# A four-layer residual block with paged attention: old rows kept together, a new passage between two parts, the end in halves, and the first tile's weights in chunks

## The chip, the cores and the metric

One core of one Trainium2 chip runs the whole program in one launch. The metric is device microseconds of one execution; the time of a kernel is the median of its runs.

## The reference

The input x has 64 sequences of 64 tokens with 512 features, float32. Four layers follow one another, each added to its input:

```
x = x + (x @ W0[id[b]] + b0[id[b]])                  # one of 16 experts for each sequence b
x = x + (x @ W1.T + scal[a] * (x @ A[a].T) @ B[a].T) # one of 8 adapters a of rank 16 for each sequence
q, k, v = x @ Wq.T, x @ Wk.T, x @ Wv.T               # 8 query heads, 4 key heads of 64
q, k = rope(rms(q)), rope(rms(k))                    # positions kv_len[b] + t
write k, v into a paged cache (blocks of 16 rows, 257 entries in the table of each sequence)
x = x + softmax(mask(q . k_cache / 16)) . v_cache @ Wo.T    # window of 256 positions
x = x + (x^T mixed over t by w3[subject[b]] (64 x 64) + bias)
```

All blocks of the table are read after all new rows are written, so a sequence can see rows that another one has just written. Products are float32 throughout.

## The kernel before

**Tiles.** The 4096 tokens are 32 tiles of 128, each of two sequences. A tile is kept once with features on partitions (for products) and once with tokens on partitions. The program is written out in order for each engine; the engines run their own instructions in that order and wait for one another where data is needed. SP issues most DMAs in program order; GpSimd (POOL) issues the gathers.

**Part 1** runs layers 0 and 1 and the q, k and v products, over groups of 1, 1, 2 and then seven times 4 tiles (`GROUPS`). For a tile, `layer0` (L254) multiplies both sequences by their expert's weights (1 MB each, `load_w0`, L237), 16 matmuls; ACT copies the result (L257), TensorE transposes it (`turn0`, L278), and DVE adds it (L279) to x plus bias, which POOL has made (`add_bias`, L265) from `biasT`, a transpose of the gathered bias rows `brow` (L683, L684). `layer1` makes the adapter's inner product (`pxa`, L630) and scales it (L635), multiplies by W1 plus the identity (L645; the identity is added to `w1` at L403), and adds the adapter's outer product (L653). The sum x2 is copied (L658), written to DRAM and transposed (`turn_x2`, L664). `product` (L141) makes q (`pq`) and k, v (`pk`). `turned` normalises and rotates q and k by `gains`, made from the sine and cosine of `rotation(o)`, eight tiles at a time (L375 to L397; 26 instructions of DVE, two of ACT). `keep_kv` writes the new k and v rows into `kvd` (L673), a compact copy of the cache in DRAM; `turn_q` (L175, L182) transposes q and writes it to `qTd`. Tile i+2 is loaded by `load_next(i)` after the first layer of tile i.

Two generators run beside this: `windows` makes the indices and masks of the cache rows that each sequence needs, and `copies` brings the 17 old blocks of each of the 64 sequences into `kvd`: 68 gathers by POOL into buffers `st` (L155, pool `op`, six buffers) and 68 writes of 512 KB by SP (L162). A write follows three gathers after its own. `other` and `layer1` advance them; up to seven gathers come in a group of four tiles. A set of 16 sequences is spread over the partitions by selection matmuls (`pw`, L488), so that one write is contiguous in DRAM.

**Passage.** Part 1 makes the q products of the first 27 tiles, and `LATE` = 6 keeps x2 of the last ones for the time after it: four products in a loop (tiles 27 to 30), the last in the first step of part 2. Meanwhile POOL gathers the cache rows of the first tiles (`load_kv`, L767, five gathers for a tile), SP loads masks (`mb`), queries (`qT`) and Wo.

**Part 2** takes one tile a step: `scores` (L839, with mask and row maximum on DVE at L847 and the exponential on ACT at L851), `attend` (L886) for the tile before, `normalise` (L859, L863), `project` (L909, residual added at L913) for the tile two before, `keys` (transposes of k and of the new rows, L820 to L827), `turn` (transposes of the weights, L872 to L876). `last(i)` does the last layer for a pair of tiles (`pz`, L921; activation with the bias, L928) and writes the output. After the loop, the last tiles are finished in the order below.

```
    last(i - 3)
    attend(i)
    project(i)
    last(i - 1)
```

## Time and profile before

| | us |
|---|---|
| median of 7 runs | 983.77 |
| runs | 978.08, 981.76, 983.44, 983.77, 984.80, 985.09, 986.80 |
| profiled execution | 988.38 |
| its span | 986.5 |
| TensorE busy | 934.1 (95%) |
| VectorE, ScalarE, GpSimd busy | 608.7, 412.5, 405.5 |
| mean granted TensorE clock | 0.986 |

The span is the time from the first to the last record on the core; all times of the profile count from its start. PE is TensorE, DVE VectorE, ACT ScalarE, POOL GpSimd, SP SyncE. `L254` is line 254 of the kernel before. In the timelines an entry has its start, its length, the operation and, in brackets, the idle time of the engine ahead of it with what ended it. The DMA share is the mean busy share of the 16 DMA engines of the core.

### The profile page before, as it was taken

The numbers are of one execution on the slowest core, as the hardware profiler recorded it, in microseconds if no ns is written. First come the engines' busy times: TensorE is split into PE (matmuls) and PEld (weight loads), VectorE is DVE, ScalarE is ACT, GpSimd is POOL, SyncE is SP. The second block draws the span as 40 slices with busy tenths as digits, with TensorE's granted clock in tenths as the row PEclk, the third lists the DMA queues.
The fourth block names the chain that finished last, engine by engine and source line by source line (L and its number), as shares of the span: only waits on it lengthen the run. The fifth ranks groups of instructions, "written<-read, shape, count | busy, mean of one in ns | idle before, by whom it ended". The sixth has DMA issues, their size and how long they took to land.

```text
span 986.5 us, 17774 instructions
## 1 busy us (share of the span) xinstructions
PE 934.1 (95%) x5393; PEld 503.8 (51%) x5393; DVE 608.7 (62%) x1737; ACT 412.5 (42%) x1082; POOL 405.5 (41%) x600
## 2 busy tenths in 40 slices
PE   3999999998999999999999589999999999999997
PEld 1444444444444444444444266666666666666663
DVE  5563988888583362542425576666666777666672
ACT  1112143222341333422223475666666666666661
POOL 2332466464353453544425443444444433333300
PEclk9899999999999999999999799999999999999999
DMA  8967999999999999999866756666665565555621
GB/s 291 305 224 263 356 370 327 403 356 352 375 313 397 385 324 406 357 361 399 297 248 216 250 179 202 201 201 200 200 197 191 181 200 186 191 183 193 201 59 43
DMA packets 133280, 260.97 MB, mean 265 GB/s; under 512 B 32801, under 2 KB 41378, under 8 KB 133186
## 3 DMA queue, kind: packets, MB, share of 16 engines
q1 hardware_dynamic: 109074, 179.66, 51.5%
q0 software_dynamic: 23280, 79.84, 24.1%
q8 instruction: 43, 0.70, 0.3%
q10 hardware_dynamic: 832, 0.35, 0.1%
q14 instruction: 51, 0.42, 0.1%
HBM read 190.29 MB, written 69.50 MB: 263 GB/s over the span
## 4 chain that ended last, share of the span: by engine, by line
PE 71%; DVE 3%; ACT 1%; DMA 1%; another core or an unknown queue 1%; issue 1%; POOL 0%; ACTq 0%; DVEq 0%
PE py L909 12%; PE ps L839 8%; PE po L886 8%; PE p L645 7%; PE pk L141 7%; PE pq L141 7%; PE p L254 6%; PE ppt L872 6%; PE pkt L820 2%; PE pz L921 2%; PE ppt L876 2%; PE pkt L826 1%; DVE pT L873 1%; PE px L664 1%; PE pqt L175 1%; PE pt L278 1%
## 5 line engine op out<-in xcount | busy, mean ns | idle before, releaser
L767 POOL DMA_INDIRECT kv<-kvd,idxn x128 | 126.4, 988 | 209.6 <-PE po L886 151.3
L851 ACT ACTIVATE pr<-pr,mx 128x320 f32<-128x320 f32 x256 | 140.1, 548 | 5.1 <-DVE mx L847 1.4
L254 PE MATMUL p<-w,xt 128*64 128x512 f32 x512 | 121.6, 612 | 13.4 <-DMA w<-in_W 13.4
L909 PE MATMUL py<-wo,oT 128*128 128x512 f32 x256 | 118.4, 605 | 1.6 <-DVE oT L904 0.8
L847 DVE CUSTOM_DVE_ANT_0 pr<-ps,mb 128x320 f32<-128x320 f32 x256 | 107.8, 486 | 14.1 <-remote 8.1
L645 PE MATMUL p<-w,x 128*128 128x512 f32 x256 | 115.6, 609 | 0.0
L141 PE MATMUL pk<-wkv,x 128*128 128x512 f32 x256 | 115.1, 594 | 0.6 <-ACT x L666 0.6
L141 PE MATMUL pq<-wq,x 128*128 128x512 f32 x256 | 115.6, 596 | 0.0
L839 PE MATMUL ps<-kT,qT 64*128 64x320 f32 x512 | 89.2, 470 | 19.2 <-DVE pT L873 10.4
L279 DVE TENSOR_TENSOR x<-pt,x 128x512 f32<-128x512 f32 x32 | 22.0, 689 | 129.5 <-PE pt L278 107.2
L136 POOL TENSOR_TENSOR qr<-qn,sq 128x512 f32<-128x512 f32 x27 | 34.3, 1269 | 157.0 <-DVE qn L135 157.0
L155 POOL DMA_INDIRECT st<-in_kvc,cidx x68 | 68.4, 1006 | 58.3 <-DMA kvd<-st 46.3
L873 DVE COPY pT<-ppt 128x512 f32<-128x512 f32 x64 | 41.6, 686 | 79.1 <-PE ps L839 37.9
L863 DVE TENSOR_SCALAR pr<-pr,sm 128x320 f32<-128x320 f32 x256 | 85.2, 394 | 2.2
L886 PE MATMUL po<-pT,kv 128*64 128x128 f32 (+1 forms) x1536 | 82.1, 278 | 0.0
L645 PEld LDWEIGHTS p<-w,x 128*128 128x128 f32 x256 | 49.0, 195 | 60.5 <-issue 59.4
L886 PEld LDWEIGHTS po<-pT,kv 128*64 128x64 f32 (+1 forms) x1536 | 68.9, 135 | 19.9 <-DVE mx L847 13.1
L909 PEld LDWEIGHTS py<-wo,oT 128*128 128x128 f32 x256 | 46.0, 189 | 62.7 <-issue 60.0
L254 PEld LDWEIGHTS p<-w,xt 128*64 128x64 f32 x512 | 34.9, 139 | 82.4 <-issue 66.5
L141 PEld LDWEIGHTS pq<-wq,x 128*128 128x128 f32 x256 | 46.5, 191 | 48.8 <-issue 47.9
L839 PEld LDWEIGHTS ps<-kT,qT 64*128 64x128 f32 x512 | 44.3, 189 | 52.9 <-DVE pT L873 29.2
L141 PEld LDWEIGHTS pk<-wkv,x 128*128 128x128 f32 x256 | 46.4, 190 | 48.5 <-issue 47.3
(186 smaller groups left out, 1313.3 us busy)
## 6 DMA issues: line engine op xcount, KB each, us to landing
w<-in_W SPq DMA_DIRECT2D x64, 1024.0 KB
kvd<-st SPq DMA_DIRECT2D x68, 512.0 KB
xt<-in_xT SPq DMA_DIRECT2D x32, 256.0 KB
x2d<-x2n SPq DMA_DIRECT2D x32, 256.0 KB
kvd<-kvn SPq DMA_DIRECT2D x32, 256.0 KB
qTd<-qTs SPq DMA_DIRECT2D x32, 256.0 KB
qT<-qTd SPq DMA_DIRECT2D x32, 256.0 KB
x2r<-x2d SPq DMA_DIRECT2D x32, 256.0 KB
```

The costliest lines, as they stand in the source:

```text
L141: TE.matmul(ps, x2s[i][:, c, :], w[:, c, :], start=c == 0, stop=c == KC - 1)
L155: P.indirect_dma_start(out=st, out_offset=None, in_=a["kvc"].rearrange("(n r) d -> n (r d)", r=2), in_offset=bass.IndirectOffsetOnAxis(ap= ...
L254: TE.matmul(p0[hs, :], xs[i][:, c, hs], w0s[i][h][:, c, :], start=c == 0, stop=c == KC - 1)
L645: TE.matmul(p1[i], x1s[i][:, c, :], w1[:, c, :], start=c == 0, stop=False)
L767: P.indirect_dma_start(out=kv[:, n, :], out_offset=None, in_=kvd, in_offset=bass.IndirectOffsetOnAxis(ap=at, axis=0),)
L839: TE.matmul(ps[g2][:, :NPOS], qT[rows, gp, b2].rearrange("p h t -> p (h t)"), kT[rows, gp, b2 * NPOS : (b2 + 1) * NPOS], start=True, stop= ...
L847: V.tensor_tensor_reduce(out=p, in0=ps[g2][:, :NPOS], in1=mb[:, b2, :], scale=-1.0, scalar=3.0e38, op0=ALU.add, op1=ALU.min, accum_out=mx[ ...
L851: S.activation(p, p, AF.Exp, bias=mx[:, g, b2 : b2 + 1], scale=-1.0, accum_out=sm[:, g, b2 : b2 + 1],)
L863: V.tensor_scalar(p, p, sm[:, g, b2 : b2 + 1], None, ALU.mult)
L872: TE.transpose(pt[:, n * 128 : (n + 1) * 128], pr[:, g, at : at + 128], ident)
L886: TE.matmul(po[b2][g2 * 64 : (g2 + 1) * 64, gp * 128 : (gp + 1) * 128], kv[rows, n, (G + g) * HD : (G + g + 1) * HD], pT[rows, c, m * 128 ...
L909: TE.matmul(py, oT[:, c].rearrange("p b t -> p (b t)"), wo[:, c, :], start=c == 0, stop=c == KC - 1)
```

## The change

It has four pieces. (1) The old rows: a gather takes, for block position j, row pair q (of four) in each half of the block, for all 64 sequences at once; no selection matmul is needed, and the 128 row pairs of a write (4 KB each) lie 136 rows (278 KB) apart in `kvd`. `op` and `xp` have five buffers instead of six. (2) The passage: `LATE` is 8, so six q products stand in the loop and two fewer in part 1; a q transpose follows the next product; the product of tile 31 stands in the first step in a bank of another pool, its normalisation in the second, and the last q transposes come in the first, fourth and fifth step. (3) The end: the projection of tile 30 uses a bank of the ring, attention of tile 31 comes ahead of the last layer of tiles 28 and 29, and projection, last layer and output of tile 31 are done in two column halves. (4) The head: the first tile's two weight blocks come in four chunks each, one block by SP's queue and one by ACT's; the transpose of the bias comes first; `rotation(0)`, the identity in `w1`, the q weights, four adapter rows and the mask (`um`, now `far`) come later.

The diff, cut:

```diff
-NSET = 4
...
-LATE = 6
+LATE = 8
...
-    cidx = const.tile([128, NSET * JOLD], I32, name="cidx")
+    cidx = const.tile([128, JOLD, BLOCK // 4], I32, name="cidx")
...
-    def product(i, w, name):
-        ps = bank(name)
+    def product(i, w, name, pool=None):
+        ps = pool.tile([128, 512], F32, name="py") if pool else bank(name)
...
-    def copies(sets, to, pool, ahead):
+    def copies(to, pool, ahead):
...
-        for s in sets:
-            for n in range(s * JOLD, (s + 1) * JOLD):
+        to = to.rearrange("(p j q r) d -> p j q (r d)", p=128, q=BLOCK // 4, r=2)
+        for j in range(JOLD):
+            for q in range(BLOCK // 4):
...
-                    in_offset=bass.IndirectOffsetOnAxis(ap=cidx[:, n : n + 1], axis=0),
+                    in_offset=bass.IndirectOffsetOnAxis(ap=cidx[:, j, q : q + 1], axis=0),
...
-                m = n - sets[0] * JOLD
-                waiting.append((to[m * 256 : (m + 1) * 256].rearrange("(p r) d -> p (r d)", r=2), st))
+                waiting.append((to[:, j, q], st))
...
-        xp = pa.enter_context(tc.tile_pool(name="xp", bufs=6))
+        xp = pa.enter_context(tc.tile_pool(name="xp", bufs=5))
...
-        op = pa.enter_context(tc.tile_pool(name="op", bufs=6))
+        op = pa.enter_context(tc.tile_pool(name="op", bufs=5))
...
-        kvi = su.tile([128, 1], I32, name="kvi")
-        tabi = su.tile([128, NBLK], I32, name="tabi")
-        for h in range(2):
-            hs = slice(h * B, (h + 1) * B)
-            nc.scalar.dma_start(kvi[hs], a["toks"][:, 3 * B :].rearrange("o b -> b o"))
-            nc.scalar.dma_start(tabi[hs], a["tab"])
...
-        def load_w0(i):
+        def load_w0(i, parts=1, queues=(nc.sync, nc.sync)):
...
-            for b in (2 * i, 2 * i + 1):
+            for b, queue in zip((2 * i, 2 * i + 1), queues):
...
-                r = nc.sync.value_load(tok1[0:1, 0, b : b + 1], min_val=0, max_val=E - 1)
-                nc.sync.dma_start(
-                    w, a["W0"][bass.ds(r, 1)].rearrange("a (c p) o -> p (a c) o", p=128)
-                )
+                r = queue.value_load(tok1[0:1, 0, b : b + 1], min_val=0, max_val=E - 1)
+                for n in range(parts):
+                    cs = slice(n * KC // parts, (n + 1) * KC // parts)
+                    queue.dma_start(
+                        w[:, cs], a["W0"][bass.ds(r, 1)].rearrange("a (c p) o -> p (a c) o", p=128)[:, cs]
+                    )
...
-        load_w0(0)
+        load_w0(0, KC, (nc.sync, nc.scalar))
...
+        load_a(0, range(2, 4))
...
-        load_weight(wq, "wqT")
-        load_a(0, range(2, 8))
+        kvi = su.tile([128, 1], I32, name="kvi")
+        tabi = su.tile([128, NBLK], I32, name="tabi")
+        for h in range(2):
+            hs = slice(h * B, (h + 1) * B)
+            nc.scalar.dma_start(kvi[hs], a["toks"][:, 3 * B :].rearrange("o b -> b o"))
+            nc.scalar.dma_start(tabi[hs], a["tab"])
...
-            for c in range(KC):
-                cs = slice(c * 128, (c + 1) * 128)
-                V.tensor_tensor(w1[:, c, cs], w1[:, c, cs], ident, ALU.add)
-
...
-        P.iota(oldr, pattern=[[0, 3], [JOLD * 256, NSET], [2, B // NSET]],
-               base=0, channel_multiplier=0, allow_small_or_imprecise_dtypes=True)
+        P.iota(oldr, pattern=[[0, 3], [JOLD * BLOCK // 2, B]], base=0, channel_multiplier=0,
+               allow_small_or_imprecise_dtypes=True)
+        half4 = su.tile([128, BLOCK // 4], F32, name="half4")
+        for h in range(2):
+            P.iota(half4[h * B : (h + 1) * B], pattern=[[1, BLOCK // 4]], base=h * BLOCK // 4, channel_multiplier=0,
+                   allow_small_or_imprecise_dtypes=True)
...
-        inset = su.tile([B, 128], F32, name="inset")
-        P.iota(inset, pattern=[[0, BLOCK // 2], [1, B // NSET]], base=0, channel_multiplier=0,
-               allow_small_or_imprecise_dtypes=True)
...
-            sel = su.tile([B, NSET, 128], F32, name="sel")
-            for k in range(NSET):
-                V.tensor_scalar(
-                    sel[:, k, :], inset, pidxf[:B], -float(k * B // NSET), ALU.subtract, ALU.is_equal
-                )
-            yield
-            yield
-            pw = bank("pw")
-            for k in range(NSET):
-                TE.matmul(pw[:, k * JOLD : (k + 1) * JOLD], sel[:, k, :], wt[:B, :JOLD], start=True, stop=True)
-            V.tensor_scalar(cidx, pw[:, : NSET * JOLD], BLOCK / 2.0, p16f, ALU.mult, ALU.add)
+            V.scalar_tensor_tensor(
+                cidx, bc(wt[:, :JOLD, None], [128, JOLD, BLOCK // 4]), BLOCK / 2.0,
+                bc(half4[:, None, :], [128, JOLD, BLOCK // 4]), ALU.mult, ALU.add,
+            )
...
-                ((4, None, ALU.logical_shift_right), 256.0),
-                ((1, BLOCK // 2 - 1, ALU.logical_shift_right, ALU.bitwise_and), 2.0 * B / NSET),
-                ((1, None, ALU.bitwise_and), 1.0),
+                ((3, 1, ALU.logical_shift_right, ALU.bitwise_and), B * JOLD * BLOCK / 2.0),
+                ((4, None, ALU.logical_shift_right), BLOCK / 2.0),
+                ((BLOCK // 2 - 1, None, ALU.bitwise_and), 1.0),
...
-        bg, old, turns, asked, made = windows(), copies(range(NSET), kvd, op, 3), {}, [], []
+        bg, old, turns, asked, made = windows(), copies(kvd[:OLD], op, 3), {}, [], []
...
-        run(rotation(0))
         scalars()
         biasT = su.tile([128, KC, B], F32, name="biasT")
-        layer0(0, False)
         pb = bank("pb")
         for c in range(KC):
             TE.transpose(pb[:, c * B : (c + 1) * B], brow[:, c * 128 : (c + 1) * 128], ident[:B, :B])
         S.copy(biasT.rearrange("p c b -> p (c b)"), pb[:, : KC * B])
-        add_bias(0)
+        layer0(0)
         turn0(0)
         load_next(0)
-
-        um = su.tile([128, NM], F32, name="um")
-        for h in range(2):
-            P.iota(um[h * 64 : (h + 1) * 64], pattern=[[1, NM]], base=0, channel_multiplier=-1,
-                   allow_small_or_imprecise_dtypes=True)
-        V.tensor_scalar(um, um, -0.5 * (WINDOW - 1), None, ALU.add)
-        V.tensor_tensor(um, um, um, ALU.mult)
-        V.tensor_scalar(um, um, 0.25 * WINDOW * WINDOW, NEG, ALU.is_gt, ALU.mult)
-        nc.sync.dma_start(maskd, um)
+        load_weight(wq, "wqT")
+        load_a(0, range(4, 8))
+
+        for c in range(KC):
+            cs = slice(c * 128, (c + 1) * 128)
+            V.tensor_tensor(w1[:, c, cs], w1[:, c, cs], ident, ALU.add)
+
+        def far():
+
+            um = su.tile([128, NM], F32, name="um")
+            for h in range(2):
+                P.iota(um[h * 64 : (h + 1) * 64], pattern=[[1, NM]], base=0, channel_multiplier=-1,
+                       allow_small_or_imprecise_dtypes=True)
+            V.tensor_scalar(um, um, -0.5 * (WINDOW - 1), None, ALU.add)
+            V.tensor_tensor(um, um, um, ALU.mult)
+            V.tensor_scalar(um, um, 0.25 * WINDOW * WINDOW, NEG, ALU.is_gt, ALU.mult)
+            nc.sync.dma_start(maskd, um)
+
         tiles = [list(range(t, t + n)) for t, n in zip(T0, GROUPS)]
...
+            if g == 0:
+                run(rotation(0))
+            elif g == 1:
+                far()
...
-            if i % 2 == 0:
+            if i % 2 == 0 or i == NT - 1:
...
+
...
-    def project(i):
-        py, oT = pyp.tile([128, 512], F32, name="py"), oTs.pop(i)
-        for c in range(KC):
-            TE.matmul(
-                py, oT[:, c].rearrange("p b t -> p (b t)"), wo[:, c, :], start=c == 0, stop=c == KC - 1
-            )
+    def project(i, ring=False, parts=1):
+        py, oT = bank("py") if ring else pyp.tile([128, 512], F32, name="py"), oTs.pop(i)
...
-        V.tensor_tensor(x3, py, pairs[i][0], ALU.add)
+        for p in range(parts):
+            fs = slice(p * D // parts, (p + 1) * D // parts)
+            if p:
+                py = bank("py")
+            for c in range(KC):
+                TE.matmul(
+                    py[:, fs], oT[:, c].rearrange("p b t -> p (b t)"), wo[:, c, fs],
+                    start=c == 0, stop=c == KC - 1,
+                )
+            V.tensor_tensor(x3[:, fs], py[:, fs], pairs[i][0][:, fs], ALU.add)
...
+    def last_one(i, parts):
+
+        x3, w3 = x3s.pop(i), pairs.pop(i)[1]
+        for p in range(parts):
+            fs = slice(p * D // parts, (p + 1) * D // parts)
+            pz = bank("pz")
+            for h in range(2):
+                hs = slice(h * T, (h + 1) * T)
+                TE.matmul(pz[hs, fs], w3[hs, :T], x3[hs, fs], start=True, stop=True)
+            res = bp.tile([128, D], F32, name="res", bufs=3)
+            S.activation(res[:, fs], pz[:, fs], AF.Identity, bias=w3[:, T:])
+            nc.sync.dma_start(out[i * 128 : (i + 1) * 128, fs], res[:, fs])
+
...
     for i in range(NT - LATE + 1, NT - 1):
         pq = product(i, wq, "pq")
+        parts[i] = parts_q(i, pq, V, cs[i])
+        next(parts[i])
         if i > NT - LATE + 2:
             turn_q(i - 2)
-        parts[i] = parts_q(i, pq, V, cs[i])
-        next(parts[i])
         if i - 1 in parts:
             run(parts.pop(i - 1))
         next(parts[i])
     keys(0)
-    turn_q(NT - 3)
     for s in range(NT):
         if s + 2 < NT:
...
             attend(s - 1)
         else:
-            pq = product(NT - 1, wq, "pq")
-        if s:
-            normalise(s, 0)
-        if s == 0:
-            run(parts.pop(NT - 2))
-            parts = parts_q(NT - 1, pq, V, cs[NT - 1])
-            normalise(s, 0)
-            next(parts)
-            next(parts)
+
+            parts[NT - 1] = parts_q(NT - 1, product(NT - 1, wq, "pq", pyp), V, cs[NT - 1])
+            turn_q(NT - 3)
+        normalise(s, 0)
+        if s == 1:
+            next(parts[NT - 1])
+            next(parts[NT - 1])
         normalise(s, 1)
         if s % 2 == 0 and s >= 4:
...
         if s + 1 < NT:
             keys(s + 1)
-        else:
-            project(s - 1)
-        if s == 0:
-            turn_q(NT - 2)
+        if s in (3, 4):
+            turn_q(NT - 5 + s)
         turn(s)
-        if s == 0:
-            run(parts)
-        elif s == 1:
-            turn_q(NT - 1)
+        if s in (2, 3):
+            run(parts.pop(NT - 4 + s))
     i = NT - 1
     load_pair(i)
     add_one(i - 1)
     add_one(i)
+    project(i - 1, ring=True)
+    attend(i)
     last(i - 3)
-    attend(i)
-    project(i)
-    last(i - 1)
+    last_one(i - 1, 1)
+    project(i, ring=True, parts=2)
+    last_one(i, 2)
```

## The prediction

> **What bounds the kernel now.** I read the page's busy times first, then the windows by stage, then TensorE's own timeline in the stages that showed gaps, then GpSimd's waits.
>
> ```profile
> PE 934.1 (95%) x5393; PEld 503.8 (51%) x5393; DVE 608.7 (62%) x1737; ACT 412.5 (42%) x1082; POOL 405.5 (41%) x600
> ```
>
> TensorE is busy for 934.1 of 986.5 us, so a change that keeps the arithmetic can only win inside the remaining 52.4 us, plus what a slow clock costs. The windows say where those lie:
>
> ```profile
> 0.00:12.00 12.00, 0.00 (x0) 0.00 (x1) 6.53 (x26) 1.28 (x1) 4.18 (x15) 1.00 0.64 181
> 12.00:30.00 18.00, 14.40 (x36) 5.47 (x37) 10.53 (x45) 1.69 (x4) 6.68 (x13) 0.84 1.05 389
> ...
> 100.00:400.00 300.00, 297.46 (x1158) 132.75 (x1156) 203.73 (x402) 88.72 (x197) 148.04 (x230) 0.99 1.00 365
> 530.00:548.00 18.00, 14.63 (x41) 6.46 (x39) 12.03 (x27) 5.87 (x16) 8.75 (x10) 1.00 0.82 276
> 548.00:560.00 12.00, 4.22 (x20) 2.59 (x22) 3.05 (x8) 2.58 (x6) 6.29 (x8) 0.58 0.84 318
> ...
> 957.00:987.00 30.00, 22.70 (x168) 12.26 (x164) 10.95 (x35) 8.77 (x23) 0.51 (x2) 0.94 0.15 44
> ```
>
> The second number is the length, the third TensorE's busy time; the last three are granted clock, DMA share and GB/s. Part 1 from 100 to 400 us leaves TensorE 2.5 us idle, with the DMA engines at a share of 1.00. The gaps are the head (12 us, then 3.6), the passage (3.4, then 7.8, with a clock of 0.58) and the end (7.3). The change touches exactly these three, and the copies inside part 1.
>
> **The head.** TensorE's timeline:
>
> ```profile
> 12.00 1.97 PE L254 MATMUL p<-w,xt 128*64 128x512 f32 x2 [12.00 <-DMA w<-in_W]
> 15.38 6.36 PE L254 MATMUL p<-w,xt 128*64 128x512 f32 x14 [1.42 <-DMA w<-in_W]
> 24.97 1.92 PE L630 MATMUL pxa<-x,ao 128*32 128x128 f32 x8 [1.89 <-DVE x L279]
> 26.82 5.82 PE L645 MATMUL p<-w,x 128*128 128x512 f32 x8
> ```
>
> A weight block is 1 MB and lands whole: the first matmul starts at 12.00 and the third waits for the second block until 15.38. Each of the 14 takes 6.36/14 = 0.454 us; sixteen of the same later take 3.65 us, 0.228 each, so this stretch runs at half rate. Then the bias: its transpose stands behind the layer's matmuls, GpSimd's addition ends after 24, and TensorE waits 1.89 us.
>
> With chunks, the two 256 KB pieces of one input chunk are enough for two matmuls. The stream does not grow: 3.1 MB had moved by 14.5 us, which holds both blocks and the tile, so the last pieces land by about 14.5 to 15. The bias rows landed at about 11 (the packets of their gather run from 9.0 to 11.0), and the transpose of the bias now comes first, so about 11.2 opens TensorE. Sixteen matmuls at half rate are 16 x 0.454 = 7.3, end 18.5, with the last pieces in time. Then copy 0.3 and transpose 0.66, addition 0.7 without the wait: layer 1's first product near 19.5 to 20 instead of 24.97, 5.2 earlier. Its eight big matmuls took 5.82 us at half rate against 3.65 later; the clock came back at 31.1, 19 us after the first matmul. Starting one earlier without the 1.42 and 1.89 gaps, it should come back inside that product; this gives up to 2.2.
>
> What is moved behind it costs something. The rotation (DVE 7.75 to 16.2, 8.45 us, until now under the wait for weights) now runs after layer 1 of tile 0, and the first steps of the index work (27.28 to 33.13, some 5.5 us with its picks) follow it on DVE, ahead of tile 1's x addition. From 20.5: 8.45 and 5.5 end at 34.5, addition 35.2. TensorE has until then the product 3.65 and 1.12, layer 0 of tile 1 3.65, two transposes 1.3, the k/v product 3.7: it would arrive at about 34 and wait 1.1. ScalarE's copy for tile 1 stands behind the sine and cosine of that rotation: another 1.0. So 5.2 + 2.2 - 2.1 = 5.3 gained by layer 1 of tile 1. Bounds: 9 if the waits are covered by the k/v product, 1 if the clock stays low through tile 0 and the bias rows land late in the fuller stream. The weight loads behind (k/v 1 MB, q 1 MB, adapter rows) are used after 38 us; the q load and four adapter loads go behind the load of tile 2, whose weights are then earlier. The DVE addition into w1 (0.9) moves behind tile 0's x addition and is needed only 1.9 us later: nothing. The mask work of 1.9 us on DVE (25.45 to 27.28) moves one group on, where DVE waited 5.7 us for TensorE at 38.8: nothing.
>
> The Trainium skill, "DMA: Bandwidth & Descriptors", Bandwidth, speaks against pieces: it asks for 1 MiB per transfer (341 GB/s) and has 138 GB/s at 64 KB. By an estimate from that page at the middle, 240 GB/s, two blocks need 8.7 us instead of 6.1, and the last pieces come 2.6 us later, at 17.5: the chain would still end at 18.4. I go by the row: several transfers share the engines, at 389 GB/s and a share of 1.05. The same page, "Issuing engines are not separate DMA queues", says that a second issuing engine saves only issue time; by the trace that is the 1.23 us between SyncE's two weight issues (3.47 and 4.70), and by that rule the second engine alone is worth at most this.
>
> **The passage.** TensorE's timeline again:
>
> ```profile
> 548.18 0.66 PE L820 MATMUL pkt<-ident,kv 128*128 128x128 f32 x4 [2.63 <-DMA kv<-kvd,idxh]
> ...
> 559.00 3.57 PE L839 MATMUL ps<-kT,qT 64*128 64x320 f32 x12 [7.29 <-ACT kT L827]
> 562.50 4.23 PE L141 MATMUL pq<-wq,x 128*128 128x512 f32 x8
> ...
> 570.73 1.25 PE L872 MATMUL ppt<-ident,pr 128*128 128x128 f32 x8 [1.59 <-DVE pr L863]
> ```
>
> The idle entries of 530 to 590 add to 14.4 us: 0.19 + 0.73 + 2.63 + 0.31 + 7.29 + 1.59 + 0.51 + 0.24 + 0.16 + 0.77. The last k/v product ended at 528.9, and the first gathered rows that needed it landed at 548.14, 19.3 us later. Between stood four q products. With LATE 8 there are six: 6 x 3.6 + 5 x 0.44 = 23.8 us, so 4.5 to spare, and the 2.63 goes. TensorE's total is unchanged, since the two products (8.1 us with their transposes) leave part 1. Each q transpose now comes behind the next product: 0.19, 0.73 and 0.31 go. The 7.29 is the doubtful one. ScalarE's copy of the keys and DVE's first masked score both start near 558.4 though their operands were ready by 552, and the burst of gathers, masks, queries and Wo (about 400 GB/s) drains at 557.8, 28.9 us after the last k/v product. If the stall belongs to the burst's end, TensorE now reaches the second scores at 23.8 + 1.1 + 1.4 = 26.3, and 2.6 of it stays. If it belongs to the old order (keys, query transpose and scores close together), all of it goes. The third case is among the rivals. The 1.59 stays, since half 1 of the normalisation of tile 1 still stands behind a q rotation with its table load, as do small ones: 3.5 altogether. Cold matmuls at 562.5 (4.23 for 3.60) give 1.0 back. Gain 14.4 - 3.5 + 1.0 = 11.9, or 9.3 with the rest of the stall. I take 10.5.
>
> **The end.**
>
> ```profile
> 965.48 3.70 PE L909 MATMUL py<-wo,oT 128*128 128x512 f32 x8 [0.78 <-DVE x L913]
> 975.72 3.70 PE L909 MATMUL py<-wo,oT 128*128 128x512 f32 x8 [0.84 <-DVE oT L904]
> 979.35 1.98 PE L921 MATMUL pz<-x,w 64*64 64x512 f32 x8
> ```
>
> From 961 on: projection of 29 3.7, turn 2.5, projection of 30 3.7 (a bank of its own, so the 0.78 goes), attention 2.6, the last layers of 28, 29 and 30 1.6 (they cover the 0.84), projection of 31 3.7 in halves, then half a last layer 0.6: about 979.3 instead of 981.35. The last activation is half of 0.69, and what follows it (982.1 to 986.5) stays. Gain 2.5; 1 if halves cost as much as wholes, 3.5 if the last activation's issue gap goes as well.
>
> **The copies.** The gathers stay 68, and so do the bytes. Four selection matmuls and DVE's wait of 3.8 us for them go, which TensorE feels as 0.6 at most. The writes are still of 4096 B per packet, 159 ns in the trace both for scattered reads and for contiguous writes, so rows 278 KB apart should cost nothing: I take 0; a tenth more per packet would be 68 x 128 x 16 ns / 16 = 8.7 us of DMA time, of which up to all shows where the share is 1.00. Five buffers instead of six:
>
> ```profile
> POOL st L155 <- DMA kvd<-st: 46.3, 12, 9.0
> ```
>
> GpSimd waits longer for a write. I put a burst 3 us later, and the x bias addition behind it has about 7.5 us to spare (it ended at 256.7 in one group and was needed at 264.2). I take 1 us in all; 5 if some groups overrun.
>
> **Sum.** 5.3 + 10.5 + 2.5 + 0.6 - 1 = 17.9. The profiled execution took 988.4 us (span 986.5), so 970.5 for one like it. It stands 4.6 above the median of 983.8; if the 7.29 stall is partly what made it long, ordinary runs gain less, so I subtract half of the 4.6: 968.
>
> **The rivals.** (a) *The stall stays* or was never in ordinary runs: the gain is 17.9 less 5.9 = 12, 972 to 976. For it: nothing in the profile names a releaser, only "remote". Against: both engines stall together while the DMA burst ends. (b) *The head does not come forward*: bias rows behind eight weight pieces, or the rotation in front of tile 1 is as long as what it freed; head gain 1, so 972 to 974. For it: DVE has 14 us of work in a row where TensorE has some 13.5. (c) *Slower: GpSimd late in part 1.* With five buffers every burst of seven gathers waits for one more write landing (7 us under load), twice in a group: 14 us against 7.5 spare, 6.5 on each of seven groups, 45 us, time near 1011. It decides when a burst ends 10.9 us later than now (7.5 spare, plus 24/7 to eat the gain and half a per cent). Against it: the longest of the present waits is 9.0 and only 12 of 68 gathers wait. (d) *The writes at a stride* hold the queue in part 1: 25% more per packet takes 22 us and cancels all; nothing in the trace prices it.
>
> **How the numbers follow.** Forecast 0.55 (962 to 972), (a) 0.17, (b) 0.10, (c) 0.09, (d) 0.04, better than 962 0.05. The measurement tells about half a per cent, 4.9 us. Faster by more: 0.82; within: 0.07, the tails of (a), (b) and (d) with part of the copies' cost; slower: 0.11, (c) and half of (d). The range 958 to 979 leaves out (c), (d) and little more.
>
> **What would show it.** Right: the bias transpose opens TensorE near 11, the first layer 1 product near 20, no wait for kv after the q products, no idle over 3 us from 530 to 590, a last layer that ends about 2 us earlier relative to the last scores. Wrong: GpSimd's wait for the writes well over 46 us with TensorE waiting for the x addition in many groups; a slow clock to 31 us and beyond; the 7.29 again at the first scores.

## The result, and the profile after

The changed kernel takes 978.39 us (median of 15 runs, 974.95 to 981.93) against 983.97 for the kernel before (36 runs, 978.08 to 989.67): a ratio of 0.9945, 95% interval 0.9928 to 0.9963. It is faster by 5.6 us, where 16 were forecast; the time lies just inside the upper end of the range. The profiled execution took 980.66 us, its span 978.6; the one of before had 988.38 and 986.5, so of the 7.7 us between these two executions 2.1 are their own distance from the medians.

The two traces, cut at four marks, say where the 7.9 us between the spans come from. The marks are the start of layer 1 of tile 1 (its `pxa`), the end of the last k/v product, the start of the fourth projection of part 2 (the first mark at which both kernels have done the same work again), and the start of the last matmul of scores. The 8.1 us are the two query products with their transposes (about 4.05 each) that the change moves from part 1 into the passage.

| stretch, us | before | after | change |
|---|---|---|---|
| start to layer 1 of tile 1 | 42.17 | 37.09 | -5.1 |
| to the end of the last k/v product | 486.68 | 480.57 | -6.1, of which -8.1 is work moved on: +2.0 |
| to the fourth projection ("the passage") | 99.72 | 106.75 | +7.0, of which +8.1 is that work: -1.1 |
| to the last scores | 329.57 | 329.40 | -0.2 |
| to the end of the span | 28.36 | 24.74 | -3.6 |

TensorE's timeline of the changed kernel, head and end (start, length, operation, idle time ahead with its releaser):

```profile
11.80 0.66 PE L671 MATMUL pb<-ident,brow 64*128 64x64 f32 x4 [11.80 <-DMA brow<-in_b,idcol]
12.39 6.04 PE L249 MATMUL p<-w,xt 128*64 128x512 f32 x16
20.65 1.09 PE L620 MATMUL pxa<-x,ao 128*32 128x128 f32 x8 [0.85 <-DVE x L274]
21.67 3.70 PE L635 MATMUL p<-w,x 128*128 128x512 f32 x8
28.55 3.65 PE L249 MATMUL p<-w,xt 128*64 128x512 f32 x14 [1.13 <-DMA w<-in_W]
...
962.39 3.60 PE L916 MATMUL py<-wo,oT 128*128 128x512 f32 x8
965.92 2.56 PE L888 MATMUL po<-pT,kv 128*64 128x128 f32 x48
969.16 1.04 PE L951 MATMUL pz<-x,w 64*64 64x512 f32 x4
970.13 3.72 PE L916 MATMUL py<-wo,oT 128*128 128x256 f32 x16
973.78 1.24 PE L951 MATMUL pz<-x,w 64*64 64x256 f32 x8
```

The bias opens TensorE at 11.80, the sixteen matmuls run without a gap, and the eight of layer 1 are at full rate (3.70 where before had 5.82). At the end no wait is left between 962 and 975.

The passage is where the forecast gain is missing. The same view there:

```profile
547.19 4.64 PE L841 MATMUL ps<-kT,qT 64*128 64x320 f32 x16 [5.00 <-ACT kT L823]
...
565.20 1.30 PE L888 MATMUL po<-pT,kv 128*64 128x128 f32 x24 [1.10 <-issue]
...
571.82 0.99 PE L874 MATMUL ppt<-ident,pr 128*128 128x128 f32 x6 [2.15 <-issue]
...
591.83 0.80 PE L841 MATMUL ps<-kT,qT 64*128 64x320 f32 x2 [1.19 <-DVE mx L849]
...
606.47 0.80 PE L841 MATMUL ps<-kT,qT 64*128 64x320 f32 x2 [1.19 <-DVE mx L849]
607.21 4.17 PE L888 MATMUL po<-pT,kv 128*64 128x128 f32 x48
```

The wait for the gathered rows is gone, as forecast. But the first scores still wait for 5 us, later steps have new waits of 1.1 to 2.2 us, and the attention at 607.21 takes 4.17 us where others take 2.56: it runs at half rate. The windows (the granted clock is the third number from the end) show that spell:

```profile
605.00:610.00 5.00, 3.81 (x35) 3.09 (x34) 4.26 (x18) 3.49 (x13) 0.00 (x0) 0.77 0.52 154
610.00:615.00 5.00, 5.00 (x36) 2.42 (x34) 3.51 (x12) 2.25 (x6) 2.67 (x3) 0.89 0.32 89
```

Two lines name what is late. ScalarE's timeline has the 5 us: its copy of a transposed query has to wait for an earlier query's write to DRAM, and the key copies of tile 0 stand behind it.

```profile
544.02 0.65 ACT L177 COPY qTs<-pqt 128x256 f32<-128x256 f32 x2 [5.54 <-DMA qTd<-qTs]
```

There are two such buffers (`qTs`). SyncE issued the writes at 531.86 and 535.16, in the middle of the burst of gathers, masks, queries and Wo:

```profile
531.86 0.41 SPq L181 DMA_DIRECT2D qTd<-qTs  x1
535.16 0.32 SPq L181 DMA_DIRECT2D qTd<-qTs  x1
```

The next copy, which needs the first of the two again, ran at 544.02, 12 us after that write was issued. VectorE's timeline has the 1.19 us:

```profile
589.16 0.75 DVE L133 TENSOR_TENSOR sq<-qn,sg 128x256 f32<-128x256 f32 x2
589.95 0.69 DVE L134 TENSOR_TENSOR qn<-qn,cg 128x512 f32<-128x512 f32 x1
590.67 0.69 DVE L135 TENSOR_TENSOR qr<-qn,sq 128x512 f32<-128x512 f32 x1
591.28 0.48 DVE L849 CUSTOM_DVE_ANT_0 pr<-ps,mb 128x320 f32<-128x320 f32 x1
```

The rotation of a late query (2.1 us, the first three lines) now stands right ahead of the mask and maximum (L849) of a step's scores; the other late rotation stands in the same place one step later. TensorE puts the scores in a ring of banks and stops until VectorE has read them. Before, both rotations ran in the first step.

### The profile page after: what moved, and what is told of

It is laid out like the page before. It is cut to its first block, busy times and chain, and to the rows that moved or that the text cites. A ratio compares the mean times of both kernels' runs of the same rounds, so it can differ in the third digit from the quotient of the medians.

```text
span 978.6 us, 17790 instructions
## 1 busy us (share of the span) xinstructions
PE 935.1 (96%) x5397; PEld 507.9 (52%) x5397; DVE 609.5 (62%) x1736; ACT 414.1 (42%) x1084; POOL 406.3 (42%) x599
## 4 chain that ended last, share of the span: by engine, by line
PE 69%; DMA 3%; DVE 2%; issue 1%; SPq 1%; ACT 1%; another core or an unknown queue 0%; POOL 0%; ACTq 0%; DVEq 0%
PE py L916 12%; PE ps L841 9%; PE po L888 8%; PE p L635 7%; PE pk L140 6%; PE ppt L874 6%; PE p L249 6%; PE pq L140 5%; PE pkt L822 2%; PE ppt L878 2%; PE pkt L828 1%; PE pz L928 1%; DMA qTd<-qTs 1%; DMA w<-in_W 1%; PE px L654 1%
## 5 line engine op out<-in xcount | busy, mean ns | idle before, releaser
L916 PE MATMUL py<-wo,oT 128*128 128x512 f32 (+1 forms) x264 | 118.3, 591 | 0.0
L635 PE MATMUL p<-w,x 128*128 128x512 f32 x256 | 112.5, 596 | 0.0
L849 DVE CUSTOM_DVE_ANT_0 pr<-ps,mb 128x320 f32<-128x320 f32 x256 | 108.1, 486 | 6.6 <-PE ps L841 4.3
L140 PE MATMUL pq<-wq,x 128*128 128x512 f32 x248 | 111.3, 593 | 0.0
L841 PE MATMUL ps<-kT,qT 64*128 64x320 f32 x512 | 92.8, 476 | 14.5 <-DVE pT L875 6.9
L888 PE MATMUL po<-pT,kv 128*64 128x128 f32 (+1 forms) x1536 | 84.2, 281 | 1.2 <-issue 1.1
L888 PEld LDWEIGHTS po<-pT,kv 128*64 128x64 f32 (+1 forms) x1536 | 70.5, 137 | 21.5 <-DVE mx L849 13.1
L135 POOL TENSOR_TENSOR qr<-qn,sq 128x512 f32<-128x512 f32 x25 | 31.7, 1269 | 109.9 <-DVE qn L134 109.9
L841 PEld LDWEIGHTS ps<-kT,qT 64*128 64x128 f32 x512 | 47.7, 193 | 48.5 <-DVE pT L875 24.5
L140 PEld LDWEIGHTS pk<-wkv,x 128*128 128x128 f32 x256 | 46.3, 190 | 49.6 <-issue 47.3
```

Of the source, the lines that this page charges most:

```text
L140: TE.matmul(ps, x2s[i][:, c, :], w[:, c, :], start=c == 0, stop=c == KC - 1)
L635: TE.matmul(p1[i], x1s[i][:, c, :], w1[:, c, :], start=c == 0, stop=False)
L841: TE.matmul(ps[g2][:, :NPOS], qT[rows, gp, b2].rearrange("p h t -> p (h t)"), kT[rows, gp, b2 * NPOS : (b2 + 1) * NPOS], start=True, stop= ...
L849: V.tensor_tensor_reduce(out=p, in0=ps[g2][:, :NPOS], in1=mb[:, b2, :], scale=-1.0, scalar=3.0e38, op0=ALU.add, op1=ALU.min, accum_out=mx[ ...
L888: TE.matmul(po[b2][g2 * 64 : (g2 + 1) * 64, gp * 128 : (gp + 1) * 128], kv[rows, n, (G + g) * HD : (G + g + 1) * HD], pT[rows, c, m * 128 ...
L916: TE.matmul(py[:, fs], oT[:, c].rearrange("p b t -> p (b t)"), wo[:, c, fs], start=c == 0, stop=c == KC - 1,)
```

## The experiments

All ratios are to the kernel before on the same chip. "Passage" is the third stretch of the table, read from one profiled execution each. It differs between executions of the same passage: 104.0 to 106.75 in four executions of the new one (the changed kernel twice, and two runs below that change the head or the end alone), and 93.55 to 99.72 in three of the old one. So a difference of a few us in it says little by itself. One chip is faster in part 2; its stretches are compared only with its own.

**Four buffers for the transposed queries.**

```diff
-        qT = late.tile([128, 2, 2, 2, T], F32, name="qTs", bufs=2)
+        qT = late.tile([128, 2, 2, 2, T], F32, name="qTs", bufs=4)
```

> The changed kernel with four buffers for the transposed queries on their way to DRAM instead of two. Theory: in the changed kernel ScalarE's copy of the third late query transpose waits 5.5 us for the write of the first one to land, and with it the key copies behind it and the first scores (5.0 us of TensorE). With four buffers that idle goes, and with it the half-rate spell of 6.8 us that follows: the first scores start about 5 us earlier after the last k/v product, the whole 5 to 7 us faster, near 972. Rival: the burst of gathers, masks, queries and Wo is what holds the first scores, whatever the copy waits for; then the wait only changes its name (mask or queries landing) and under 2 us are gained, 977 to 979.

973.32 us against 979.28, ratio 0.9931 (0.9912 to 0.9949). The first scores wait 0.44 us for the keys instead of 5.00, so the two buffers were that wait. The passage is 102.14 instead of 106.75 (or 104.0, the shortest of the new passage); 2.43 us stand at a query transpose that waits for VectorE. In the time this is 0.1% better than the changed kernel's 0.9945, which the intervals don't tell apart.

**The rotations moved as well.**

```diff
+        if s in (0, 2):
+            run(parts.pop(NT - 2 + s // 2))
         if s in (3, 4):
             turn_q(NT - 5 + s)
         turn(s)
-        if s in (2, 3):
-            run(parts.pop(NT - 4 + s))
```

> Four buffers as above, and the rotations of the last two late queries stand on VectorE ahead of the weights' transposes of the first and the third step, where it sits idle 2.4 and 3.3 us, instead of right ahead of the scores of the third and fourth step. Theory: each of these rotations (2.1 us) holds the mask and maximum of the next scores, 1.19 us of TensorE each, and brings a half-rate spell of 3.4 us; both idles and one spell go: 3 to 4 us less than with four buffers alone. Rival: VectorE is merely the last of several in those steps (the exponentials and the copies follow at once), and under 1 us changes.

964.78 us against 979.28, ratio 0.9857 (0.9837 to 0.9878). The passage is 93.67 us, 13.1 below the changed kernel's. Its TensorE timeline:

```profile
541.93 3.33 PE L841 MATMUL ps<-kT,qT 64*128 64x320 f32 x16 [1.11 <-ACT kT L823]
...
564.07 1.42 PE L874 MATMUL ppt<-ident,pr 128*128 128x128 f32 x8 [2.05 <-DVE pr L865]
...
579.74 1.93 PE L841 MATMUL ps<-kT,qT 64*128 64x320 f32 x12 [0.81 <-ACT pT L875]
```

The waits of 5.00 and 1.19 are gone, and the window from 535 to 600 has no cold stretch:

```profile
535.00:600.00 65.00, 59.41 (x465) 39.32 (x465) 53.70 (x175) 45.19 (x126) 31.23 (x35) 1.00 0.69 221
```

The gain over four buffers alone (973.32 to 964.78 in the time on one chip, 8.5 us in the passage too) is more than twice what I expected. In the passage 2.3 of it lie ahead of the first scores, before any step that this edit touches, so 6.2 are the edit's by these two executions: the two idles of 1.19 us, a spell at half clock of 3.4 us that followed one of them, another at 567.1, and smaller waits.

**The rotations alone**, with two buffers (the same edit without the first):

> The changed kernel with only the two rotations moved ahead of the weights' transposes (first and third step), the transposed queries in two buffers as in the change. Theory: the rotations and the buffers are separate waits. The rotations' part (two idles of 1.19 us and the half-rate spells behind them) goes, the 5 us of ScalarE behind the write of the first query stay: some 4 us more than with four buffers and the rotations moved, ratio to before near 0.990. Rival: the two buffers cost nothing that is not hidden elsewhere, since four buffers alone brought under 1 us in the median: then this is as fast as with four buffers, 0.986.

971.67 us against 980.59, ratio 0.9908 (0.9880 to 0.9936); passage 99.95, and the first scores wait 5.77 us for the keys. So the two waits are separate. In the passage, against 106.75, the buffers give 4.6 us, the rotations 6.8 and both 13.1; against 104.0 it is 1.9, 4.1 and 10.3. That the buffers matter in the time as well is likely, since the intervals of 0.9908 and 0.9857 just fail to meet; but these two ratios are from two chips, and one other kernel's ratio moved by 0.0031 between chips (0.9913 and 0.9882, next).

**The old passage, all else as changed** (LATE 6, order of before), run on two chips, the second time beside the changed kernel.

> The changed kernel with the passage of before (LATE 6, the order of before up to the second step), head, copies and end as changed. If the prediction's sum for the passage were right, this would be about 10 us slower than the changed kernel, 988. By the two traces the new passage gave about 1 us and took 2.5 us from the last group of part 1, so: within 2 us of the changed kernel, 976 to 980.

970.90 us, ratio 0.9913 (0.9894 to 0.9932), passage 98.83 with two products fewer. At its ratio of 0.9945 the changed kernel would take 973.9 on this chip, so the old passage is some 3 us faster, more than the 2 that I allowed.

> The kernel with the old passage once more, as the reference on one chip for the next one. Theory: its first scores stand 6 to 7 us behind a release that the profile does not name, as in the kernel before. Rival: on a chip where the loads land sooner there is no such stand.

> The changed kernel on the same chip. Theory: its passage (last k/v product to fourth projection, two late products more) is within 2 us of the old one on the same chip, after 8.1 us for these products are taken off; ScalarE's wait for the write of a query is there again. Rival (the prediction's sum): 10 us shorter.

On one chip: old passage 972.95 us, ratio 0.9882 (0.9837 to 0.9927); changed kernel 979.71, ratio 0.9938 (0.9918 to 0.9958). So the new passage makes the kernel slower, by 6.8 us here. By the traces of this pair the passage is 93.55 + 8.1 = 101.6 against 104.6, 3.0 of it, and part 1 between its marks 486.36 - 8.1 = 478.3 against 481.7, another 3.4. I had expected the passages within 2 us, and 6 to 7 us of standing at the first scores of the old one. The old passage's trace on this chip also says what the 7.29 us of the kernel before were worth:

```profile
542.25 1.12 PE L822 MATMUL pkt<-ident,kv 128*128 128x128 f32 x4 [3.68 <-DMA kv<-kvd,idxh]
547.75 0.81 PE L841 MATMUL ps<-kT,qT 64*128 64x320 f32 x4 [0.86 <-issue]
...
557.26 1.26 PE L874 MATMUL ppt<-ident,pr 128*128 128x128 f32 x8 [2.67 <-DVE pr L865]
```

The wait at the first scores, 7.29 us before and 6.02 in the first run of the old passage, is 0.86 here, with the same order of instructions. It is no fixed cost of the old passage. ("issue" means that the engine waited for nothing that the profile shows.)

The traces say more about the release that the profile calls "remote". In the kernel before it is this:

```profile
558.36 0.59 ACT L827 COPY kT<-pkt 128x512 f32<-128x512 f32 x1 [5.89 <-remote]
558.47 0.49 DVE L847 CUSTOM_DVE_ANT_0 pr<-ps,mb 128x320 f32<-128x320 f32 x1 [8.12 <-remote]
```

Both engines wait here for TensorE's own semaphore; VectorE had passed its waits for DMAs by 550.43. The semaphore steps at 551.97 and then only at 558.34, 558.40, 558.44 and 558.48, though by the records' ends, which are modelled, the transposes and first scores that it counts were done by 551.72. In the first run of the old passage four steps come from 550.59 to 550.74 for work that ends by 545.23; in the second run they follow the work within 0.1 us. So what came late was TensorE's report of finished work. Why it came late is not shown.

**The old passage with half of the burst issued later**, also on two chips:

```diff
-    for i in range(2):
-        load_kv(i)
-        load_q(i)
-        load_mask(i)
+    load_kv(0)
+    load_q(0)
+    load_mask(0)
...
-    nc.sync.dma_start(wo, a["woT"].rearrange("(c p) f -> p c f", p=128))
-    load_q(2)
...
+        if s == 0:
+            after_keys(0)
+            scores(0)
+            load_kv(1)
+            load_q(1)
+            load_mask(1)
+            nc.sync.dma_start(wo, a["woT"].rearrange("(c p) f -> p c f", p=128))
+            load_q(2)
```

> The old passage (LATE 6) with head, copies and end as changed, but the gathers, masks and queries of tile 1, Wo and the queries of tile 2 are issued after the first scores instead of before them. Theory: the 6 to 7 us that the first scores stand still in the old order (VectorE's first masked score and ScalarE's key copy released by a queue that the profile does not name) are a wait for the whole burst of loads to land, since the first writes into part 2's tiles wait for DMA queues of all lanes; with about half of the burst issued later the burst ahead of the scores drains before TensorE comes, and the 6 us go, though the gathers of tile 1 may then make step 1 wait for up to as much. Rival: the stall has another cause (the same place in the order of the engines) and stays at 6 us at the first scores.

952.83 us against 961.12, ratio 0.9901 (0.9869 to 0.9934). No wait stands at the first scores; the second keys wait 3.27 us for their rows. That chip runs the steady part of part 2 in 314 us instead of 327 to 330, so its times and stretches are compared only with its own.

> The old passage with the loads for tile 1, Wo and the queries of tile 2 issued after the first scores, on the same chip as the old passage. Theory: the stand of 6 to 7 us at the first scores is the wait for the burst and goes; the gathers of tile 1 come later and cost about 3 us at the second keys: from the last k/v product to the fourth projection 3 to 4 us less, the time 3 us less. Rival: the stand is tied to the order of the engines: it stays, and with the 3 us at the second keys this is slower.

977.08 us, ratio 0.9908 (0.9870 to 0.9946): not better than the old passage beside it (0.9882), passage 99.82 against 93.55. The wait at the first scores is absent in both, so the pair cannot tell whether the burst made it. That stays open.

**LATE 6 alone in the changed kernel.**

> The changed kernel with LATE 6 and nothing else: four late query products in the loop, two more inside the last group of part 1. Theory: the two products were filler in the last group (its tiles lose 0.6 us each and one 1.2 us without them), so 2.5 us come back there; in the passage the gathered rows come 3 us after TensorE is ready for them, the wait that the two products were moved to hide. Both cancel: within 2 us of the changed kernel. Rival: as the prediction had it, the two products cover the wait at no cost, and this is 3 to 5 us slower.

972.61 us, ratio 0.9928 (0.9909 to 0.9946), passage 97.77. From the mark in tile 1 to the last k/v product it takes 486.62 us, 478.5 without the two products, 2.0 less than the changed kernel; the keys wait 4.13 us in the passage, where 3 were expected. LATE 8 neither gains nor loses beyond the intervals. This stretch also clears the copies: with them as changed and LATE as before, it is as long as before (486.62 and 486.68).

**LATE 7 with both repairs.**

> Four buffers and the rotations moved, with LATE 7: five late products instead of six. Theory: the product put back is filler in the last group of part 1 (about 1.2 us come back there), and five products (20 us) still just cover the 19 us until the gathered rows land: 1 us less than with LATE 8, ratio near 0.985. Rival: the first keys now wait for the rows, and it is 1 to 3 us more.

946.57 us against 961.12, ratio 0.9843 (0.9817 to 0.9869), as expected: the best kernel here, though not apart from the one with LATE 8 by its interval. The mean granted clock is 1.000, and the keys wait 0.25 us for the rows. Its passage is 85.65 us; the new passage without the repairs takes 100.1 on this chip (in the run with both blocks on one queue), of which 4.05 are the sixth product. So on one chip, too, the two repairs shorten it by some 10 us.

**The last tile's root moved to the first step.**

Against the kernel with four buffers and the rotations moved:

```diff
         normalise(s, 0)
-        if s == 1:
-            next(parts[NT - 1])
-            next(parts[NT - 1])
         normalise(s, 1)
...
             project(s - 2)
+        if s == 0:
+            next(parts[NT - 1])
+            next(parts[NT - 1])
         if s + 1 < NT:
             keys(s + 1)
-        if s in (0, 2):
-            run(parts.pop(NT - 2 + s // 2))
+        if s in (2, 3):
+            run(parts.pop(NT - 4 + s))
```

> Four buffers, the first steps of the last tile's query (square, root with its table, scaling) in step 0 after the normalisation instead of between the halves of the normalisation in step 1, and the two rotations ahead of the weights' transposes of the third and fourth step. Theory: the 2.05 us that TensorE waits in step 1 for the second half of the normalisation stand behind that query's root; they go, and nothing is late in step 0, where ScalarE and VectorE each sit idle over 2.4 us: 2 us less than with the rotations moved alone, ratio near 0.984. Rival: the table load moves the key copies of step 0 back by the same amount, and nothing changes.

971.82 us, ratio 0.9902 (0.9873 to 0.9931): slower than expected. The 2.05 us are gone, but the next scores wait 1.74 us for ScalarE's copy of the transposed weights (`pT`), a half-rate spell of 3.4 us comes back at 562.7, and the passage is 95.69. The edit moves the rotations too, so the run does not tell the two moves apart.

**Whole weight blocks.**

```diff
-        load_w0(0, KC, (nc.sync, nc.scalar))
+        load_w0(0, 1, (nc.sync, nc.scalar))
```

> The changed kernel with the first tile's two weight blocks whole (1 MB each, still from two queues). Theory: the pieces let the first layer run while the rest lands; with whole blocks its second matmul waits until about 14.5 us, the first layer ends near 21 instead of 18.4, and layer 1 of tile 0 starts 2.5 to 3 us later, all of which reaches the second tile. Rival (a page of the Trainium skill asks for large transfers): whole blocks land earlier than pieces and layer 1 starts within 1 us of the change.

980.09 us against 980.59, ratio 0.9992 (0.9971 to 1.0013).

```profile
13.72 1.97 PE L249 MATMUL p<-w,xt 128*64 128x512 f32 x2
18.83 5.30 PE L249 MATMUL p<-w,xt 128*64 128x512 f32 x14 [3.14 <-DMA w<-in_W]
26.32 1.09 PE L620 MATMUL pxa<-x,ao 128*32 128x128 f32 x8 [0.85 <-DVE x L274]
```

Layer 1 of tile 0 starts 5.7 us later than with the pieces (26.32, not 20.65), layer 1 of tile 1 3.8 (40.89, not 37.09; the other runs with pieces have 35.4 to 36.8). 1.3 of the 5.7 are the bias rows, which open TensorE at 13.13 instead of 11.80. The pieces are what most of the head's gain rests on. The Trainium skill ("DMA: Bandwidth & Descriptors", Bandwidth) asks for transfers of 1 MiB; here four of 256 KB beat one of 1 MB, since TensorE can begin with the first.

**Both blocks on one queue.**

```diff
-        load_w0(0, KC, (nc.sync, nc.scalar))
+        load_w0(0, KC, (nc.sync, nc.sync))
```

> The changed kernel with the chunks of both weight blocks on SyncE's queue. Theory: the second block's chunks are issued after all of the first's, so TensorE's second matmul waits for about four more issues of 0.4 us and for the first block to land; layer 1 of tile 0 starts 2 to 4 us later. Rival (the Trainium skill's page on DMA: several issuing engines save only issue time): under 1.3 us.

956.05 us against 961.12, ratio 0.9936 (0.9912 to 0.9959), as the changed kernel. TensorE waits once more for a weight piece:

```profile
13.55 5.51 PE L249 MATMUL p<-w,xt 128*64 128x512 f32 x14 [1.48 <-DMA w<-in_W]
```

Layer 1 of tile 0 starts at 21.25, against 18.89 to 20.88 in three runs with two queues on this chip (the old passage with the later burst, LATE 7, and the four buffers for the old rows). That is less than my 2 to 4 us, in part because the bias rows landed 1.5 us or more earlier (9.51). Layer 1 of tile 1 starts at 35.81, against 35.69 to 36.18: by then the second queue has brought nothing that shows, which agrees with the skill's "Issuing engines are not separate DMA queues" on the same page.

**The old end.**

```diff
+        else:
+            project(s - 1)
...
-    project(i - 1, ring=True)
-    attend(i)
-    last(i - 3)
-    last_one(i - 1, 1)
-    project(i, ring=True, parts=2)
-    last_one(i, 2)
+    last(i - 3)
+    attend(i)
+    project(i)
+    last(i - 1)
```

> The changed kernel with the end of before (last layer of tiles 28 and 29, attention, projection whole, last layer whole). Theory: from the end of the last scores to the end of the span the change took 3.6 us off (28.0 to 24.4); with the old end these come back, in the trace and in the time. Rival: the reordering alone or the halves alone did nothing and another stage gave the time: under 1 us.

978.88 us against 980.59, ratio 0.9982 (0.9964 to 1.0001). From the last scores to the end it takes 27.80 us, 3.1 more than the change.

**Four buffers for the old rows.**

```diff
-        op = pa.enter_context(tc.tile_pool(name="op", bufs=5))
+        op = pa.enter_context(tc.tile_pool(name="op", bufs=4))
```

> The changed kernel with four buffers for the old rows on their way instead of five. It tests the prediction's slower rival, that GpSimd's waits for these writes reach TensorE through the x bias additions. With five buffers those waits doubled (46.3 to 89.8 us) and TensorE's time through part 1 did not change. Theory: the writes have slack, the waits grow again (over 120 us) and part 1 loses under 2 us. Rival: the slack is used up at four, and each of seven groups pays 1 to 4 us: 7 to 28 us more than the change.

1079.83 us against 961.12, ratio 1.1215 (1.1175 to 1.1256). GpSimd's waits for the writes (us in total, times, longest), in the changed kernel and in this one:

```profile
POOL st L155 <- DMA kvd<-st: 89.8, 27, 6.8
```

```profile
POOL st L155 <- DMA kvd<-st: 216.4, 34, 13.9
```

With five buffers the waits had doubled from before (46.3 us) and TensorE felt next to nothing; with four they reach it. The path is not the x bias addition that I named, for which VectorE waits 14.5 us in all. It is the products of gain and sine (`sg`, in `gains`) that GpSimd makes behind its gathers: VectorE's rotations wait for them, ScalarE waits for VectorE, and TensorE for ScalarE's copy. First VectorE's wait in the changed kernel, then the same here, then TensorE's here:

```profile
DVE sq L133 <- POOL sg L110: 34.8, 36, 3.5
```

```profile
DVE sq L133 <- POOL sg L110: 152.2, 38, 16.5
PE pt L273 <- ACT s L252: 99.3, 16, 12.8
```

The clock falls as well (0.945 on the mean). My theory of ample slack was wrong, and the rival's 7 to 28 us were far too few. By the order of the program, a write follows three gathers after its own, so with four buffers a gather needs the buffer of a write that was only just issued.

## Why the prediction was wrong

*The head* (5.3 forecast) gave 5.1, but not by all of its terms. The bias rows were the gate (11.2 forecast, 11.80) and the layer was done by 18.4. Its sixteen matmuls took 6.04 us, not 7.3. Layer 1 of tile 0 started 4.3 us earlier, where 5.2 were forecast. Its eight matmuls ran at full rate and saved 2.1 (2.2 forecast), but not because a clock came back 19 us after the first matmul: before, the granted clock was 1.00 until 24 us and 0.55, 0.50 and 0.81 in the three stretches of 3 us from there; after, it is 1.00 throughout the head. So the slow matmuls ahead of 24 us, which I read as half rate, were not the granted clock either; no run says what slowed them. The two waits forecast for tile 1, behind the rotation on VectorE and ScalarE, did not come; 1.13 us for tile 1's weights did, and some 1.1 in slower matmuls of its first layer. That the sum came out is in part luck.

*The end* (2.5) gave 3.6, 3.1 against the old end with all else equal. The last matmul ends 2.0 us earlier behind the last scores, about as forecast; the other 1.1 to 1.6 lie behind it, in a stretch that I had left unchanged.

*The copies* (0.6 - 1) cost nothing that TensorE felt. The threshold that I put at a burst 10.9 us later was not reached at five buffers; one buffer further the kernel is slower by 12%, on another path than the one I priced. Strided writes show no price: the 8704 packets of 4 KB that write the old rows took 162.8 ns on the mean before and 161.6 after, and from 100 to 400 us TensorE is busy for 297 us in both kernels.

*The passage* (10.5) is the step that failed. It gave 1.1 in the two profiled executions, and part 1 lost 2.0 by it; by the runs on one chip the new passage costs 6.8 us against the old. The step was wrong in four places.

First, I counted the idle entries of one profiled execution as if every one paid them. The 7.29 us at the first scores were in that execution and not in another of the same order, on another chip; the sum took them off nearly whole, with half of 4.6 us as the only discount. I also wrote that their operands were ready by 552; that rests on modelled ends, and TensorE's semaphore reported the work at 558.3. What held it back stays open.

Second, I read the edit as "each transpose one product later, hence no wait" and did not follow where each transpose's output goes: all transposes share two buffers whose writes stand in the burst, so ScalarE stopped until one had landed (5.00 us of TensorE in both executions of the changed kernel, 0.44 with four buffers).

Third, I costed the moved rotations at nothing. They were removed from a step in which TensorE waited anyway and put ahead of the scores of two steps in which VectorE is what TensorE waits for (1.19 us each in the first execution, 0.86 and 1.18 in the second; one of the four waits was followed by a half-rate spell). Moving them away took 8.5 us off the time with four buffers.

Fourth, part 1 lost about 2 us, since the two moved products had filled gaps in its last group; I had costed that at zero. With LATE 6 they come back.

Put right (four buffers, rotations elsewhere) the passage is 10 to 13 us shorter than the change's: that the room was there was right, and what fills it was not.

*The rivals.* (a), the stall stays, comes nearest: 5.00 us at the same place, but with another releaser, and the time is longer than its 972 to 976. (b) and (d) did not happen, nor did (c). The chance for a faster kernel was put on the right side; the gain's interval reaches from 0.4% to 0.7%, at the edge of what I called measurable. That the time lies inside the range at all is owed to its width.

## What to carry to other kernels

An idle entry in one profiled execution is a price only if other executions have it: where no releaser is named, count it with a chance, not as gain. When a piece of work is moved, list for the new place which engine is awaited there, and for each output how many buffers it has and what has to land before they come free; two rotations of two microseconds each, on the engine that is awaited, were worth 8.5 here. Buffers taken away can cost nothing down to a step and then a great deal (six and five here, then four): compare their number with the distance between a gather and its write.

## What the runs showed of the hardware

The granted clock can fall to half after short gaps. In the changed kernel it is at half for 3.4 us from 607.7 on, just after an idle of 1.19 us, while the same idle at 590.6 had no such effect; with the root moved to the first step such a spell follows waits of at most 1.13 us, and with the rotations moved none follows a wait of 2.05. What decides is not settled here. The cost shows: the attention under the spell at 607.7 took 4.17 us instead of 2.56.

A write can take long to land in a burst. The 256 KB of transposed queries issued at 531.86 held their buffer until just before 544.02, with the DMA engines at a share of 0.99 from 535 to 540.

Chips differ: the kernel before took 961.1 us on one chip, and 979.3, 980.6 and 985.6 on three others. Ratios carry over better: two kernels that ran on two chips had 0.9913 and 0.9882, and 0.9945 and 0.9938.
